# Layer norms between attention units: a subtraction and multiplication moved to GpSimd, its quarters set three half chunks apart

## The chip, the cores and the metric

The kernel runs on one core of a Trainium2 chip. The metric is the device time of one execution in microseconds (us), as the median of several runs. Durations inside the execution are from one profiled execution of the kernel before.

## What is computed

Two transformer layers over four sequences (batches) of 512 tokens with 320 features each. Every layer is self attention, cross attention on a context of 1601 tokens with 192 features, and a gated feed-forward part, each with a layer norm ahead and a residual behind. All is float32; there are 20 heads of 16 features.

```python
def _ln(x, g, b):
    m = jnp.mean(x, axis=-1, keepdims=True)
    v = jnp.mean(jnp.square(x - m), axis=-1, keepdims=True)
    return (x - m) * jax.lax.rsqrt(v + EPS) * g + b
...
h1 = _ln(x, n1_g, n1_b)
x = _attn(h1, h1, q1, k1, v1, o1_w, o1_b, heads) + x
h2 = _ln(x, n2_g, n2_b)
x = _attn(h2, context, q2, k2, v2, o2_w, o2_b, heads) + x
h3 = _ln(x, n3_g, n3_b)
proj = h3 @ ff_w1 + ff_b1
a, g = jnp.split(proj, 2, axis=-1)
ff = a * jax.nn.gelu(g, approximate=False) @ ff_w2 + ff_b2
return ff + x
```

## The kernel before

The attention work is cut into units: one layer, one kind (self or cross), one batch and one group of four heads, so five units a batch. A unit goes through its keys in **chunks** of 128: 4 chunks in self attention, 13 in cross attention (the last of 65 keys). For a chunk, TensorE makes the scores of the four heads (`st`, L1282, twelve matmuls with the row of negative maxima `nrows` as the third pass), ScalarE takes the exponentials (`pr`, L1292), TensorE multiplies them with the values one chunk later (`av`, L1308, four matmuls in the program, eight in the trace), ScalarE copies that out (`vo`, L1327) and GpSimd adds it to the unit's sum `o` (L1328). Since every query's maximum must be known before the exponentials, the scores of the **next** unit are made at the same time in another layout (`sps`, L1054, eight matmuls a chunk) and VectorE reduces them to maxima (`pm` and `nmax`, L1069, four a chunk). The two kinds of matmul use different rows of TensorE and run beside each other; products whose keys or queries have not been moved into place in time are left out of a chunk and made up later as a round of their own (`round_of(extra[0])`).

Everything else is fitted between the chunks by a planner that runs while the program is built: values (`vps`, L1015), keys of the context (`kps`, L951), queries (`qps`, L927), output projections (`ops`, L1211), and the norms. Each such step stands in a chain (a queue that is taken in order) with a cost, a due round, and two tests; one chunk advances the clock by two rounds, so a round is half a chunk. `pick` takes the chain whose head is due first, `steps` runs heads as credit allows and at most one or two steps marked `LIGHT` after a chunk. The planner also keeps an estimate of when each engine is free (`busy`), from which `bank` picks PSUM banks and `taken` picks VectorE or ScalarE for a copy out of PSUM.

A norm (`add_norm`) is such a list of steps in the chain "norm": `stats` (a quarter, 128 tokens, at a time), `root` (the inverse root, mostly on GpSimd), then for each quarter `normalise` (L562, 128x320, written to the only buffer `hn`) and `blocks` (L568, VectorE's transpose of 32x32 blocks from `hn` into `hturned`), then `spread`, which queues the DMAs (L578) that carry `hturned` to `hT`, one band each, on SyncE's queue; and in the chain "scale" `affine` (L595, GpSimd). Only then is `hT` handed over, and the step `hold` at the head of the projection chain waits for that; behind it in the same chain stand the queries of that batch's first unit and the keys and queries of the units after it. Three kinds of norm differ: with `first` set they take another path (`plain`, L608, and TensorE's transposes); feed-forward norms of the batches 1 to 3 run their quarters in pairs; all others go by `normalise` and `blocks` in one step per quarter. Before the change, a quarter's `normalise` is directly followed by its `blocks` on VectorE, four steps in four rounds.

`max_end` makes a unit's row of negative maxima at the end of the unit before; in cross attention its four DMAs (`rows`, L1133) are not issued at once but put at the head of a list of errands, which `carry` works off after a chunk.

Of the kernel before, what the change touches and what calls it, by code (L numbers as in the profile page):

```python
# [24 lines left out]
NQ = N // P  # L25
# [50 lines left out]
def kernel(ctx: ExitStack, tc: tile.TileContext, x, context, ws, out):  # L76
# [18 lines left out]
    nc = tc.nc  # L95
# [199 lines left out]
    class Unit:  # L295


        def __init__(self, l, kind, b, g):
            self.l, self.kind, self.b, self.g = l, kind, b, g
            self.cross = kind == "cross"  # L300
            self.nkeys = S2 if self.cross else N
            self.nch = (self.nkeys + P - 1) // P

            self.moves = {"k": deque(), "q": deque()}
            self.moving = {"k": 0, "q": 0}
            self.open = 6 if self.cross else 3
            self.keyed = None
            self.when = None
            self.vmade = [0, 0]

            self.made = {"q": 0, "k": 0, "kv": 0}
            self.scored = 0
            self.valued = 0
            self.steps = 2 * self.nch if kind != "ff" else 2 * NHC + NQ
            self.before = None
            self.others = []
            self.early = False
            self.own = {}
            self.pairs = self.hT = self.kvT = None
# [63 lines left out]
    clock = {"round": 0, "credit": 0.0, "lights": 0, "tiles": None, "ff": False}  # L383
    ALIKE = ("project", "early", "proj", "values")
    LIGHT = 0.01
# [26 lines left out]
    def busy(engine, us, *tiles):  # L412
        expect[engine] = max([expect[engine]] + [bank_of[id(t)][3] + 0.05 for t in tiles]) + us
        for t in tiles:
            bank_free[bank_of[id(t)][0]] = expect[engine] + 0.09
# [12 lines left out]
    def add(chain, cost, f, due, ready=yes, soon=yes):  # L428
        chains[chain].append((cost if isinstance(cost, tuple) else (cost,), due, ready, soon, f))
# [107 lines left out]
    def add_norm(l, b, i, put, done, due):  # L537
        xb = xs[b]
        s = {}

        def stats(t):
            if t == 0:
                hn_used.append(b)
                s["mv"] = two.tile([P, NQ, 2], F32, tag="mv", name="mv")
            st = three.tile([P, 6], F32, tag="st6", name="st6")
            nc.vector.bn_stats(st, xb[:, t, :])
            nc.vector.bn_aggr(s["mv"][:, t, :], st)
            busy("dve", 0.65)
# [9 lines left out]
        def normalise(t):  # L558
            if t == 0:
                s["turned"] = one.tile([P, DB, NQ, SLOT], F32, tag="hturned", name="hturned")  # L560
            s["hn"] = one.tile([P, D], F32, tag="hn", name="hn")
            nc.vector.tensor_scalar(  # L562
                s["hn"], xb[:, t, :], s["mv"][:, t, 0:1], s["rstd"][:, t : t + 1], ALU.subtract, ALU.mult,
            )
            busy("dve", 0.4)

        def blocks(t):
            nc.vector.transpose(s["turned"][:, :, t, :], s["hn"])  # L568
            busy("dve", 0.45)
            s["round"] = clock["round"]  # L570
# [66 lines left out]
        ahead = 0 if first or i == 2 and b else EARLIER  # L637
# [5 lines left out]
        def later(n, key="round"):  # L643
            return lambda: clock["round"] >= s[key] + n

        def together(f):
            return [lambda ts=ts: [f(t) for t in ts] for ts in (((0, 1), (2, 3)) if i == 2 and b else ((0,), (1,), (2,), (3,)))]
# [12 lines left out]
        if first:  # L660
# [5 lines left out]
                    may_overwrite if k == 0 else yes, later(1),  # L666
                )
            return
        for t, f in enumerate(together(lambda t: (normalise(t), blocks(t)))):
            add("norm", LIGHT, f, due - ahead - 13 + t, yes, yes if t else later(1))  # L670
        add("norm", 0.0, spread, due - ahead - 6, may_overwrite, later(1))

        def there(k):
# [106 lines left out]
    errands = deque()  # L780
# [333 lines left out]
    def max_end(u):  # L1114

        top, high, low = (u.nm[:, :, i, :] for i in range(3))
        nc.vector.tensor_reduce(
            high.bitcast(F32R), top.rearrange("p j (t o) -> p j t o", o=1), AX.X, ALU.max, negate=True
        )
        nc.vector.tensor_reduce(  # L1120
            low, u.nm[:, :, 0:2, :].rearrange("p j e t -> p j t e"), AX.X, ALU.add, negate=True
        )
        turned = two.tile([P, SLOT], F32, tag="turned", name="turned")

        nc.vector.transpose(turned.rearrange("p (j c) -> p j c", j=HG), u.nm[:, :, 1:3, :].rearrange("p j e t -> p j (e t)"))
        busy("dve", 0.6)
        slots = u.rows.bitcast(F32).rearrange("(g s) n -> s g n", s=DH)[0].rearrange("g (t r) -> g t r", t=NQ)

        def rows():
            for i in range(P // SLOT):  # L1130
                part = slice(i * SLOT, (i + 1) * SLOT)
                queue = (nc.sync, nc.scalar, nc.gpsimd, nc.sync)[i] if start["on"] else nc.sync
                queue.dma_start(out=slots[:, :, part], in_=turned[part, :])  # L1133

        if u.cross and u.before.cross:
            errands.appendleft((clock["round"] + 1, yes, rows))
        else:
            rows()
# [133 lines left out]
    def main(u, give, nxt):  # L1272

        pr, raised = {}, {}

        def score(c, j):
            r = min(P, u.nkeys - c * P)
            rows = slice(j * SLOT, (j + 1) * SLOT)
            own = []

            def product(e):
                nc.tensor.matmul(  # L1282
                    own[0][:r, :],
                    lhsT=ones[rows, :r] if e == 2 else u.keys(rows, c),
                    rhs=u.rows[rows, :] if e == 2 else u.q[rows, e, :],
                    start=(e == 0),
                    stop=(e == 2),
                )

            def exponential():  # L1290
                p = prs.tile([P, N], F32, tag="pr", name="pr")
                nc.scalar.activation(p[:r], own[0][:r], AF.Exp)  # L1292
                pr[c, j] = p
                busy("act", 0.515, *own)
                raised[c] = expect["act"]

            return (j,), [lambda e=e: product(e) for e in range(3)], exponential, own, lambda: own.append(bank("st"))
# [34 lines left out]
        for c in range(u.nch):  # L1332
# [29 lines left out]
            if not last and c == u.nch - 3:  # L1362
                max_reduce(nxt)
                max_end(nxt)
# [52 lines left out]
    def ff_main(u, give, nxt):  # L1417
        done = 0

        def beside(room, n):  # L1420

            nonlocal done
            if room:
                for extra in give(done, True)[1]:
                    round_of(extra)
            done += n
            if done == u.steps - 1 and nxt is not None and nxt.kind != "ff":
                max_reduce(nxt)
# [302 lines left out]
```

## Time and profile before

| | |
|---|---|
| Median of 3 runs | 2983.01 us (2982.85 to 2983.1) |
| Profiled execution, its time | 2982.2 us |
| Its span, first to last instruction | 2980.4 us |
| What lies around the span | 1.8 us |
| TensorE busy, share of the span | 2874.4 us, 96% |
| VectorE, ScalarE, GpSimd busy | 2119.6, 1889.8, 1193.4 us (71, 63, 40%) |
| Granted TensorE clock, mean | 0.994 |

Engines are named PE (TensorE), DVE (VectorE), ACT (ScalarE), POOL (GpSimd) and SP (SyncE, the DMA queue). A row of the timeline has the start in us from the span's begin, the duration, engine, line, operation, the tiles written and read, a count if like instructions are merged, and in brackets how long the engine had been idle and what ended that. A row of a grouped view has the count, then busy us and mean ns of one, then the idle time ahead with its causes.

### The profile page before, as it was taken

How to read it: one execution, taken by the hardware profiler on the slowest of the kernel's cores; microseconds unless marked ns; L12 is line 12 of the kernel's file. 1: busy time of each engine (PE TensorE's matmuls, PEld its weight loads, DVE VectorE, ACT ScalarE, POOL GpSimd, SP SyncE). 2: the span in 40 equal slices, each digit the busy share in tenths (PEclk: the TensorE clock that was granted, in tenths of full speed). 3: DMA queues.
4: the chain of work that ended last, by engine and by line, in shares of the span. 5: the costliest groups of instructions: out<-in, count | busy, mean ns of one | idle time of the engine just before them, and what ended most of it. 6: DMA issues, size and time to landing. Idle time of an engine off the chain costs nothing.

```text
span 2980.4 us, 84363 instructions
## 1 busy us (share of the span) xinstructions
PE 2874.4 (96%) x35018; PEld 1511.5 (51%) x35018; DVE 2119.6 (71%) x4143; ACT 1889.8 (63%) x3746; POOL 1193.4 (40%) x1305
## 2 busy tenths in 40 slices
PE   8999999999999999999999899999999999999999
PEld 4455555555554555355554555555555555544555
DVE  7877888889889888323268778888898888873221
ACT  3766677877877878501137676778878778784000
POOL 3445344554544545211224443445445454451110
PEclk8999999999999999999999999999999999999999
DMA  4443233132132122200123342221221121222000
GB/s 105 104 125 97 71 80 95 49 89 60 48 91 68 39 56 61 83 17 14 38 60 73 92 100 68 61 61 48 62 64 46 49 71 42 55 56 77 23 22 14
DMA packets 186543, 188.70 MB, mean 63 GB/s; under 512 B 69668, under 2 KB 137264, under 8 KB 186160
## 3 DMA queue, kind: packets, MB, share of 16 engines
q1 hardware_dynamic: 185368, 182.11, 24.2%
q8 instruction: 276, 4.52, 0.6%
q10 hardware_dynamic: 760, 1.18, 0.2%
q14 instruction: 107, 0.88, 0.1%
q0 software_dynamic: 32, 0.00, 0.0%
HBM read 55.76 MB, written 29.36 MB: 29 GB/s over the span
## 4 chain that ended last, share of the span: by engine, by line
PE 79%; DVE 16%; ACT 1%; DMA 1%; issue 1%; POOL 1%; SPq 0%; ACTq 0%; POOLq 0%; DVEq 0%
PE av L1308 22%; PE st L1282 16%; PE fps L1393 9%; DVE pm L1069 8%; PE sps L1054 6%; PE yps L1500 6%; PE vps L1015 5%; DVE nmax L1069 4%; PE kps L951 4%; PE ops L1211 3%; PE qkps L886 3%; PE fps L1453 2%; PE qps L927 2%; PE sps L1081 1%; ACT pr L1292 1%; DVE hturned L608 1%
## 5 line engine op out<-in xcount | busy, mean ns | idle before, releaser
L1292 ACT ACTIVATE pr<-st 128x512 f32<-128x512 f32 (+1 forms) x2720 | 1405.1, 603 | 418.3 <-PE st L1282 382.4
L1069 DVE TENSOR_REDUCE pm<-sps 128x1 f32<-128x512 f32 x1920 | 1187.2, 682 | 136.3 <-PE sps L1054 125.8
L1328 POOL TENSOR_TENSOR o<-o,vo 128x512 f32<-128x512 f32 x576 | 740.3, 1285 | 1101.8 <-ACT vo L1327 1091.9
L1054 PE MATMUL sps<-kT,q 32*128 32x512 f32 x4800 | 866.5, 429 | 12.2 <-DMA q<-low 3.2
L1308 PE MATMUL av<-pr,vals 128*32 128x512 f32 (+1 forms) x5440 | 735.1, 606 | 72.3 <-DVE nmax L1069 18.5
L1282 PE MATMUL st<-q,kT 32*128 32x512 f32 (+1 forms) x5120 | 791.6, 421 | 1.3 <-DVE pm L1069 0.8
L1282 PEld LDWEIGHTS st<-q,kT 32*128 32x128 f32 (+1 forms) x5120 | 420.7, 180 | 289.7 <-issue 119.1
L1282 PE MATMUL st<-nrows,ones 32*128 32x512 f32 (+1 forms) x2720 | 542.5, 400 | 8.5 <-DMA nrows<-turned 8.5
L1054 PEld LDWEIGHTS sps<-kT,q 32*128 32x128 f32 x4800 | 423.4, 184 | 93.3 <-DVE nmax L1069 15.7
L1069 DVE TENSOR_REDUCE nmax<-sps 128x1 f32<-128x512 f32 x640 | 395.7, 681 | 85.9 <-PE sps L1054 83.0
L1327 ACT COPY vo<-av 128x512 f32<-128x512 f32 x576 | 352.4, 612 | 20.9 <-PE av L1308 19.9
L1464 ACT ACTIVATE gl<-fps,b 128x512 f32<-128x512 f32 x80 | 54.8, 687 | 414.3 <-PE fps L1453 303.0
L1308 PEld LDWEIGHTS av<-pr,vals 128*32 128x32 f32 (+1 forms) x5440 | 111.1, 108 | 347.2 <-DVE pm L1069 179.4
L1393 PE MATMUL fps<-hT,w 128*128 128x512 f32 x640 | 283.2, 597 | 0.0
L1282 PEld LDWEIGHTS st<-nrows,ones 32*128 32x128 f32 (+1 forms) x2720 | 246.7, 180 | 33.2 <-issue 7.2
L1465 DVE SCALAR_TENSOR_TENSOR hid<-fps,b,gl 128x512 f32<-128x512 f32 x80 | 59.7, 748 | 238.8 <-ACT gl L1464 236.7
L1393 PEld LDWEIGHTS fps<-hT,w 128*128 128x128 f32 x640 | 119.2, 190 | 155.1 <-issue 151.8
L1500 PE MATMUL yps<-w,hid 128*128 128x320 f32 x640 | 176.0, 435 | 0.1
L1500 PEld LDWEIGHTS yps<-w,hid 128*128 128x128 f32 x640 | 120.4, 190 | 56.5 <-ACT gl L1464 5.3
L1211 PEld LDWEIGHTS ops<-wo,aT 112*32 112x32 f32 (+1 forms) x3072 | 97.7, 110 | 64.1 <-issue 42.9
L1211 PE MATMUL ops<-wo,aT 112*32 112x160 f32 (+1 forms) x3072 | 125.9, 300 | 0.9 <-DVE pm L1069 0.7
L886 PE MATMUL qkps<-hT,wqk 96*32 96x256 f32 (+1 forms) x1920 | 121.3, 395 | 0.0
(89 smaller groups left out, 2340.2 us busy)
## 6 DMA issues: line engine op xcount, KB each, us to landing
kT<-stages SPq DMA_DIRECT2D x160, 200.2 KB
oway<-o SPq DMA_DIRECT2D x80, 256.0 KB
q<-high SPq DMA_DIRECT2D x160, 64.0 KB
q<-low SPq DMA_DIRECT2D x160, 64.0 KB
kT<-high SPq DMA_DIRECT2D x60, 128.0 KB
q<-high SPq DMA_DIRECT2D x60, 128.0 KB
kT<-low SPq DMA_DIRECT2D x57, 128.0 KB
aT<-oway SPq DMA_DIRECT2D x32, 224.0 KB
```

The source lines that it names most:

```text
L886: nc.tensor.matmul(ps[f : f + m, :w], lhsT=wqk[:n, k, f // GD, column : column + m], rhs=first.hT[:n, k, at : at + w], start=(k == 0), sto ...
L1015: nc.tensor.matmul(ps[f : f + m, :w], lhsT=u.kvT[:n, k, at + f : at + f + m], rhs=wv[:n, k, h0 * DH : h1 * DH], start=(k == 0), stop=(k == ...
L1054: nc.tensor.matmul(ps, lhsT=u.q[j * SLOT : (j + 1) * SLOT, e, t * P : (t + 1) * P], rhs=u.kT[j * SLOT : (j + 1) * SLOT, u.k0 + s * 512 : u ...
L1069: nc.vector.tensor_reduce(to[:, j : j + 1], ps, AX.X, ALU.max)
L1211: nc.tensor.matmul(ps[f : f + m, : D // 2], lhsT=aT[:n, k, f * NQ + t * SLOT : f * NQ + t * SLOT + m], rhs=wo[:n, k, cols], start=(k == 0) ...
L1282: nc.tensor.matmul(own[0][:r, :], lhsT=ones[rows, :r] if e == 2 else u.keys(rows, c), rhs=u.rows[rows, :] if e == 2 else u.q[rows, e, :], ...
L1292: nc.scalar.activation(p[:r], own[0][:r], AF.Exp)
L1308: nc.tensor.matmul(ps[j * SLOT : (j + 1) * SLOT, :], lhsT=columns_of[:r, head : head + SLOT], rhs=pr.pop((c, j))[:r, :], start=True, stop= ...
L1327: nc.scalar.copy(vo, ps)
L1328: nc.gpsimd.tensor_tensor(u.o, u.o, vo, ALU.add)
L1393: nc.tensor.matmul(ps, lhsT=w1[:, k, i * FF + c * P : i * FF + (c + 1) * P], rhs=natural(u.hT[:, k]), start=start, stop=stop,)
L1500: nc.tensor.matmul(ps[:, :D], lhsT=hid[c][:, t * P : (t + 1) * P], rhs=w2[:, c, :], start=(c == 0), stop=(c == NHC - 1),)
```

## The change

For cross attention's norms of the batches 1 to 3 and the feed-forward norm of batch 0, in both layers (eight norms, `alone` false), `normalise` goes to GpSimd. It becomes a step of its own, free of charge and not `LIGHT`, due three rounds after the one before; `blocks` is a step of its own, due two rounds behind its `normalise` and held until two rounds have passed. `spread` follows as before. The estimate for VectorE is no longer charged for the moved instruction. Besides, a unit's `rows` still waiting among the errands is carried out at the latest when its `main` begins.

```diff
@@ def add_norm
+        alone = i == 2 and b > 0 or i == 0
...
             s["hn"] = one.tile([P, D], F32, tag="hn", name="hn")
-            nc.vector.tensor_scalar(
+            (nc.vector if alone else nc.gpsimd).tensor_scalar(
                 s["hn"], xb[:, t, :], s["mv"][:, t, 0:1], s["rstd"][:, t : t + 1], ALU.subtract, ALU.mult,
             )
-            busy("dve", 0.4)
+            if alone:
+                busy("dve", 0.4)
+            s["round"] = clock["round"]
...
-        for t, f in enumerate(together(lambda t: (normalise(t), blocks(t)))):
-            add("norm", LIGHT, f, due - ahead - 13 + t, yes, yes if t else later(1))
+        if alone:
+            for t, f in enumerate(together(lambda t: (normalise(t), blocks(t)))):
+                add("norm", LIGHT, f, due - ahead - 13 + t, yes, yes if t else later(1))
+        else:
+            for t in range(NQ):
+                add("norm", 0.0, lambda t=t: normalise(t), due - ahead - 17 + 3 * t, yes, later(1))
+                add("norm", LIGHT, lambda t=t: blocks(t), due - ahead - 15 + 3 * t, yes, later(2))
         add("norm", 0.0, spread, due - ahead - 6, may_overwrite, later(1))
@@ def max_end
         if u.cross and u.before.cross:
+            u.rows_of = rows
             errands.appendleft((clock["round"] + 1, yes, rows))
@@ def main
         pr, raised = {}, {}
+        for todo in [e for e in errands if e[2] is u.rows_of]:
+            errands.remove(todo)
+            todo[2]()
```

What this does to the order on the engines, at three places. (Lines of the changed kernel are counted in its own file: its L564, L572, L1003, L1063, L1078, L1228, L1295, L1321, L1341 are L562, L568, L994, L1054, L1069, L1218, L1282, L1308, L1328 of before.)

VectorE at the norm of batch 2 ahead of layer 0's cross attention, before; `hn` is the normalised quarter, `hturned` its transposed blocks, `pm<-sps` the reductions of a chunk:

```order
L994 COPY vals<-vps 128x12x16
L733 STREAM_TRANSPOSE stages<-stages 128x6x32
L562 TENSOR_SCALAR hn<-x_109,mv,root_12657 128x320
L568 STREAM_TRANSPOSE hturned<-hn 128x10x32
L1069 TENSOR_REDUCE pm<-sps 128x1 x4
L562 TENSOR_SCALAR hn<-x_109,mv,root_12657 128x320
L568 STREAM_TRANSPOSE hturned<-hn 128x10x32
L1069 TENSOR_REDUCE pm<-sps 128x1 x4
L994 COPY vals<-vps 128x12x16
L562 TENSOR_SCALAR hn<-x_109,mv,root_12657 128x320
L568 STREAM_TRANSPOSE hturned<-hn 128x10x32
L1069 TENSOR_REDUCE pm<-sps 128x1 x4
```

And VectorE at the same norm after the change:

```order
L742 STREAM_TRANSPOSE stages<-stages 128x6x32
L1078 TENSOR_REDUCE pm<-sps 128x1 x4
L572 STREAM_TRANSPOSE hturned<-hn 128x10x32
L1228 TENSOR_TENSOR x_107<-ops,x_107 128x160
L1078 TENSOR_REDUCE pm<-sps 128x1 x8
L572 STREAM_TRANSPOSE hturned<-hn 128x10x32
L1078 TENSOR_REDUCE pm<-sps 128x1 x4
L1003 COPY vals<-vps 128x12x16
L1078 TENSOR_REDUCE pm<-sps 128x1 x4
L1003 COPY vals<-vps 128x12x16
L572 STREAM_TRANSPOSE hturned<-hn 128x10x32
L1078 TENSOR_REDUCE pm<-sps 128x1 x4
```

`hn` is gone from VectorE, and the transposes stand two chunks (eight reductions) apart where they stood one apart.

GpSimd at the same norm after the change; `o<-o,vo` is the addition of one chunk, `high` and `low` belong to a query's move:

```order
L1341 TENSOR_TENSOR o<-o,vo 128x512
L564 TENSOR_SCALAR hn<-x_109,mv,root_12609 128x320
L1341 TENSOR_TENSOR o<-o,vo 128x512 x2
L564 TENSOR_SCALAR hn<-x_109,mv,root_12609 128x320
L812 COPY high<-low 128x256
L813 TENSOR_TENSOR low<-low,high 128x256
L1341 TENSOR_TENSOR o<-o,vo 128x512 x2
L564 TENSOR_SCALAR hn<-x_109,mv,root_12609 128x320
L1341 TENSOR_TENSOR o<-o,vo 128x512 x2
L564 TENSOR_SCALAR hn<-x_109,mv,root_12609 128x320
```

Each `hn` stands right behind a chunk's addition, and there are two additions from one `hn` to the next; the transposition of a quarter stands behind the four reductions of the following chunk.

TensorE late in the cross attention of batch 0 in layer 0, before, one chunk; `sps<-kT_135,q_104` are the products for the maxima of batch 1's first unit, whose queries come out of the first changed norm:

```order
L1308 MATMUL av<-pr,vals 32x512 x4
L951 MATMUL kps<-ctxT,w_116 32x200 x8
L1282 MATMUL st<-q_102,kT_134 128x512 x2
L1054 MATMUL sps<-kT_135,q_104 128x512 x2
L1282 MATMUL st<-q_102,kT_134 128x512 x2
L1054 MATMUL sps<-kT_135,q_104 128x512 x2
L1282 MATMUL st<-nrows_98,ones 128x512 x2
L1282 MATMUL st<-q_102,kT_134 128x512 x4
L1054 MATMUL sps<-kT_135,q_104 128x512 x2
L1282 MATMUL st<-nrows_98,ones 128x512 x2
L1054 MATMUL sps<-kT_135,q_104 128x512 x2
```

The same place after the change, this chunk and the two behind it:

```order
L1321 MATMUL av<-pr,vals 32x512 x4
L1295 MATMUL st<-q_102,kT_134 128x512 x8
L1295 MATMUL st<-nrows_98,ones 128x512 x4
L1321 MATMUL av<-pr,vals 32x512 x4
L1295 MATMUL st<-q_102,kT_134 65x512 x8
L1295 MATMUL st<-nrows_98,ones 65x512 x4
L1321 MATMUL av<-pr,vals 32x512 x4
L1295 MATMUL st<-q_103,kT_101 128x512 x8
L1295 MATMUL st<-nrows_97,ones 128x512 x4
```

Three chunks have lost their `sps` products; they come back as a second set of eight in three later chunks. The queries of that batch (`qps`) stand three chunks later than before. At the same norm of layer 1 it is one chunk that loses them and one that has sixteen. On the DMA queue, the four DMAs of `nrows`, which stood between the DMAs of `hT` in these norms, now stand ahead of them.

More of the change, by code (lines that the diff above doesn't have):

```diff
@@ L300, in __init__ @@
             self.cross = kind == "cross"
+            self.rows_of = None
             self.nkeys = S2 if self.cross else N
```

## The prediction

> **What bounds the kernel now.** I read the page first, then the chain of waits inside eight stretches, then the timeline of one of them engine by engine.
>
> ```profile
> PE 2874.4 (96%) x35018; PEld 1511.5 (51%) x35018; DVE 2119.6 (71%) x4143; ACT 1889.8 (63%) x3746; POOL 1193.4 (40%) x1305
> PE 79%; DVE 16%; ACT 1%; DMA 1%; issue 1%; POOL 1%; SPq 0%; ACTq 0%; POOLq 0%; DVEq 0%
> ```
>
> TensorE is the bound: 2980.4 - 2874.4 = 106 us of the span are all that it is idle. VectorE has 16% of the chain that ended last, so where TensorE waits it is mostly VectorE that it waits for, and an instruction taken from VectorE is worth something only in chunks where VectorE falls behind. How the moved instruction and the transposition that stays behave over the whole run (min/median/max in ns):
>
> ```profile
> L562 DVE TENSOR_SCALAR hn<-x,mv,root x64: 426/446/1507, 496.7 to 2876.6; 128x320 f32<-128x320 f32 x64
> L568 DVE STREAM_TRANSPOSE hturned<-hn x64: 510/511/513, 497.1 to 2877.1; 128x320 f32<-128x320 f32 x64
> ```
>
> The transposition takes 0.51 us always. `hn` takes 0.43 to 1.51 us, the same work each time. The timeline of GpSimd and then of VectorE at the norm of batch 2 in layer 0 shows why:
>
> ```profile
> 704.64 1.29 POOL L1328 TENSOR_TENSOR o<-o,vo 128x512 f32<-128x512 f32 x1
> ...
> 708.41 1.29 POOL L1328 TENSOR_TENSOR o<-o,vo 128x512 f32<-128x512 f32 x1 [2.48 <-ACT vo L1327]
> ```
>
> ```profile
> 704.84 1.27 DVE L562 TENSOR_SCALAR hn<-x,mv,root 128x320 f32<-128x320 f32 x1
> ...
> 708.95 0.93 DVE L562 TENSOR_SCALAR hn<-x,mv,root 128x320 f32<-128x320 f32 x1
> ...
> 710.35 2.44 DVE L1069 TENSOR_REDUCE pm<-sps 128x1 f32<-128x512 f32 x4
> ```
>
> The first `hn` began 0.20 us into GpSimd's addition and ended at 706.11, 0.18 us behind its end (705.93); the second began 0.54 us into the next one and ended 0.18 us behind it (709.88 against 709.70). `hn` waits on VectorE until GpSimd's addition is over, with four reductions queued behind it. What that costs TensorE, by the starts of its `av` matmuls, one group a chunk:
>
> ```profile
> 706.44 1.06 PE L1308 MATMUL av<-pr,vals 128*32 128x512 f32 x8 [0.22 <-ACT pr L1292]
> ...
> 711.05 1.07 PE L1308 MATMUL av<-pr,vals 128*32 128x512 f32 x8 [0.89 <-DVE pm L1069]
> ...
> 714.35 1.06 PE L1308 MATMUL av<-pr,vals 128*32 128x512 f32 x8 [0.22 <-ACT pr L1292]
> ...
> 718.24 1.07 PE L1308 MATMUL av<-pr,vals 128*32 128x512 f32 x8
> ```
>
> The three chunks last 4.61, 3.30 and 3.89 us. The first and the third hold `qps` and `ops` beside the usual matmuls. The same chunks where no norm runs, first with `qps`, then with `ops`:
>
> ```profile
> 539.56 1.06 PE L1308 MATMUL av<-pr,vals 128*32 128x512 f32 x8
> ...
> 543.38 0.64 PE L1308 MATMUL av<-pr,vals 128*32 128x512 f32 x4
> ```
>
> ```profile
> 384.08 1.06 PE L1308 MATMUL av<-pr,vals 128*32 128x512 f32 x8
> ...
> 387.42 1.07 PE L1308 MATMUL av<-pr,vals 128*32 128x512 f32 x8
> ```
>
> They last 3.82 and 3.34 us, so this norm costs 0.79 + 0.55 = 1.3 us.
>
> **What goes.** Eight norms lose four `hn` each. For all eight stretches together (busy us, the second row for L562 alone):
>
> ```profile
> sum 130.00, PE 119.06 PEld 58.54 DVE 126.01 ACT 95.25 POOL 58.90; mean PE 14.88 PEld 7.32 DVE 15.75 ACT 11.91 POOL 7.36
> ```
>
> ```profile
> sum 130.00, DVE 27.13; mean DVE 3.39
> ```
>
> 27.1 us leave VectorE, which is busy for 126.0 of the 130. TensorE is idle there for 130.00 - 119.06 = 10.9 us: the lower bound of what they cost. It is not all, since matmuls that are held up in their middle count as busy, so I take the lengths of the chunks. The worst chunk of the first norm and of the last, and a bare chunk (nothing beside scores, products and `av`) for comparison:
>
> ```profile
> 502.47 1.07 PE L1308 MATMUL av<-pr,vals 128*32 128x512 f32 x8
> ...
> 507.05 0.64 PE L1308 MATMUL av<-pr,vals 128*32 128x512 f32 x4
> ```
>
> ```profile
> 2620.69 1.07 PE L1308 MATMUL av<-pr,vals 128*32 128x512 f32 x8
> ...
> 2625.50 1.07 PE L1308 MATMUL av<-pr,vals 128*32 128x512 f32 x8
> ```
>
> ```profile
> 582.62 1.06 PE L1308 MATMUL av<-pr,vals 128*32 128x512 f32 x8
> ...
> 585.35 0.64 PE L1308 MATMUL av<-pr,vals 128*32 128x512 f32 x4
> ```
>
> The first is a bare one: 4.58 instead of 2.73, 1.85 too long. The last holds one `vps` of 192 columns, as the one from 711.05 does: 4.81 instead of 3.30, 1.51 too long. Subtracting so, chunk by chunk, the norms cost 2.1, 1.3, 1.6, 2.2, 2.0, 1.7, 1.8 and 2.2 us, together **-14.9 us** if all of it goes.
>
> **What stays.** The 32 transpositions stay on VectorE, now two chunks apart. What such a load costs is seen just ahead of the first norm:
>
> ```profile
> 492.98 0.36 DVE L994 COPY vals<-vps 128x192 f32<-128x192 f32 x1
> 493.26 0.37 DVE L733 STREAM_TRANSPOSE stages<-stages 128x192 f32<-128x192 f32 x1
> 494.27 2.48 DVE L1069 TENSOR_REDUCE pm<-sps 128x1 f32<-128x512 f32 x4 [0.65 <-PE sps L1054]
> ```
>
> With 0.7 us beside its reductions VectorE still had to wait 0.65 us for TensorE: nothing lost. Only in a bare chunk do 2.44 + 0.51 = 2.95 us exceed its 2.73, by 0.2; about one cross chunk in five or six is bare, so six of 32 make **+1.2 us**. From above: if the transpositions go on costing what norm work costs now, 14.9 us for 27.1 busy us of `hn` and 32 x 0.51 = 16.4 of transposing, it is 0.34 x 16.4 = 5.6. From below, nothing.
>
> **What GpSimd gets.** The trace has no 128x320 `TENSOR_SCALAR` there, but two others:
>
> ```profile
> L595 POOL TENSOR_SCALAR hT<-hT,lng,lnb 128x512 f32<-128x512 f32 x32 | 24.7, 772 | 127.6 <-DMA hT<-hturned 116.0 <-PE ops L1211 11.6
> L513 POOL TENSOR_SCALAR root<-root 128x4 f32<-128x4 f32 x22 | 5.1, 231 | 258.2 <-DVE root L507 257.9
> ```
>
> Between 0.23 and 0.77; on the line through both it is 0.57 us, 18 us in all. GpSimd was idle 2.48 us ahead of the addition at 708.41, so I cost it at **0**. An `hn` behind that addition would end at 709.70 + 0.57 = 710.27, and the transposition stands behind the next four reductions, which ended at 712.79, or with VectorE no longer late some 1.2 us sooner (they could start when their products do): a cover of 1.3 to 2.5 us.
>
> **What is moved.** The last quarter is turned some four chunks later, so `spread`, the twelve DMAs of `hT` (sixteen for feed-forward), `affine`, and with them `hold`, come later too. Most norms have room for it; the first cross norm of each layer has not. There the queries come three chunks later in layer 0, and three chunks lose their products for the maxima, which return as a second set in three later chunks; in layer 1 it is one. What one costs, by a chunk that lost them, then one that has a second set and the one behind it, then an ordinary chunk with the same `vps` of 128 columns:
>
> ```profile
> 766.58 1.07 PE L1308 MATMUL av<-pr,vals 128*32 128x512 f32 x8
> 768.47 1.07 PE L1308 MATMUL av<-pr,vals 128*32 128x512 f32 x8
> ```
>
> ```profile
> 395.11 1.06 PE L1308 MATMUL av<-pr,vals 128*32 128x512 f32 x8
> ...
> 399.34 1.06 PE L1308 MATMUL av<-pr,vals 128*32 128x512 f32 x8
> ...
> 402.92 1.06 PE L1308 MATMUL av<-pr,vals 128*32 128x512 f32 x8
> ```
>
> ```profile
> 533.64 1.06 PE L1308 MATMUL av<-pr,vals 128*32 128x512 f32 x8
> ...
> 536.60 0.64 PE L1308 MATMUL av<-pr,vals 128*32 128x512 f32 x4
> ```
>
> The second set with its aftermath costs 7.81 - 2 x 2.96 = 1.89. The chunk without gives back 2.73 - 1.89 = 0.84 if it stands alone, but little when three stand in a row, because ScalarE needs its time for them:
>
> ```profile
> 768.57 2.07 ACT L1292 ACTIVATE pr<-st 128x512 f32<-128x512 f32 x4
> 770.50 0.62 ACT L1327 COPY vo<-av 128x512 f32<-128x512 f32 x1
> ```
>
> 2.07 + 0.62 = 2.69, as long as a bare chunk. So four at 1.05 to 1.89 are 4.2 to 7.6 us; three of the four stand in a row, so I take **+6.0**. The other shifts exchange the places of `vps`, `kps` and `ops` chunk for chunk, at zero.
>
> **The row of maxima.** Its four DMAs now go ahead of those of `hT`, which delays no one, and once, in batch 0 of layer 0, ahead of the last loads of the division; there TensorE waited for them. All eight such waits:
>
> ```profile
> PE st L1282 <- DMA nrows<-turned: 8.5, 8, 2.4
> ```
>
> One of eight is worth at most about 1.1 us and at least nothing; I take **-0.5**. The flush in `main` changes nothing else in the order.
>
> **The sum** is -14.9 + 1.2 + 0 + 6.0 - 0.5 = -8.2 us, made against the profiled execution: 2980.4 us of span and 1.8 around it are 2982.2, and become 2974.0. The median of the runs lies 0.8 us higher (2983.0), so I forecast **2974.8 us**. With each term at its better bound it is 2971.2 (-14.9 + 0 + 4.2 - 1.1), at its worse 2985.3 (-10.9 + 5.6 + 7.6).
>
> **The rivals.**
> - *The late products cost nothing*, because the chunks with a second set fall where TensorE's other work hides it: -14.9 + 1.2 - 0.5, 2968.8 us. For it speaks that such chunks with `qps` or `ops` in the next absorb part; against it the 1.89 measured, and that the heavy chunks are now bunched ahead of them. 0.12.
> - *The stall stays in part*: only TensorE's visible idle time comes back (-10.9) and the transpositions keep 5.6: 2983.2 with the order's 6.0. For it: VectorE is 97% busy in these stretches, and it loses only 27.1 of 126.0. 0.18.
> - *Slower: the transposition waits for GpSimd.* VectorE works in order; behind the transposition stand four reductions, behind these TensorE's next products. If GpSimd delivers `hn` late, by a burst of additions and the splits of 1.2 to 2.5 us that stand in the same queue, every late us goes to TensorE. 32 delays of 0.26 us eat the 8.2 us, 0.44 us each make it 2989. Against it: the cover of 1.3 us or more. 0.08, at 2990.
> - *The load is only moved, the interference with it.* Then the 14.9 does not come, the order's 6.0 and 18 us of GpSimd work do: about 2989. Against it: the 64 transpositions, many of them beside GpSimd's work, all took 0.51 us, so what remains on VectorE there does not wait for GpSimd. 0.05. The Trainium skill, Perfetto Trace Analysis, section Optimizing Scalar/DVE Operations, speaks for this rival: it says that VectorE and GpSimd share a read port, and that offloading from the one to the other might therefore not help; by that rule the time would be this 2989. The trace agrees with the sharing (`hn` ends 0.18 us behind the addition), but what is moved here is the very instruction that waits.
>
> That the instruction would not be moved is excluded by the order.
>
> **How the numbers follow.** The forecast's case has a chance of 0.55, the four rivals 0.43, and 0.02 is left for what I don't see. About 0.2% (6 us) is what a measurement of this kernel can tell from no change: faster means below 2977.0. Of the forecast's case three quarters lie there, of the first rival all, of the second a sixth: 0.41 + 0.12 + 0.03 = 0.56. Slower by 6 us are most of the last two and what is left: 0.11. Within: 0.33. The range of 8 in 10 takes in the first rival at its low end and the second at its high end: 2968.5 to 2983.5.
>
> **What would show it.** In the profile after, no `hn` on VectorE in the eight stretches and 32 on GpSimd at 0.5 to 0.6 us; the chunk with `qps` at batch 2 down from 4.61 to some 3.8 us; TensorE's idle time there down by 10 us. At the first cross norm of layer 0, three chunks without `sps`, 2 to 2.7 us each, and three of 4.3 us. Wrong would be: waits of VectorE's transposition for GpSimd's `hn`; chunks of the norms still over 4 us; or a long wait of `sps` for the DMAs of queries and keys behind the first norm, which I have put at nothing since those products are only taken two chunks after the DMAs' issue.

## The result, and the profile after

The changed kernel takes 2973.13 us (median of 7 runs, 2967.84 to 2974.48), the kernel before beside it 2982.85 (7 runs): a ratio of 0.9966, 95% interval 0.9954 to 0.9977, 9.7 us less. The forecast was 2974.8. The total was right, but two of the terms that make it up were wrong by 4.5 and 6 us, in opposite directions, and so was the reason given for the largest.

TensorE still bounds: 99.4 us of the span are all that it is idle, 106 before (busy us and share of the span by engine):

```profile
span 2971.5 us, 84372 instructions
...
PE 2872.1 (97%) x35018; PEld 1511.8 (51%) x35018; DVE 2088.6 (70%) x4103; ACT 1891.4 (64%) x3754; POOL 1239.0 (42%) x1337
```

The moved normalisation (min/median/max in ns), and below it what the transpositions waited for (us, times):

```profile
L564 POOL TENSOR_SCALAR hn<-x,mv,root x32: 1428/1440/1453, 498.8 to 2630.8; 128x320 f32<-128x320 f32 x32
...
  POOL hn L564: 1.0, 3
```

On GpSimd it takes 1.44 us, two and a half times my estimate, and costs next to nothing all the same: 29 of 32 transpositions found it done. The norm of batch 2 in layer 0, on GpSimd, VectorE and TensorE:

```profile
708.77 1.29 POOL L1341 TENSOR_TENSOR o<-o,vo 128x512 f32<-128x512 f32 x1 [1.84 <-ACT vo L1340]
710.04 1.45 POOL L564 TENSOR_SCALAR hn<-x,mv,root 128x320 f32<-128x320 f32 x1
```

```profile
711.63 0.50 DVE L572 STREAM_TRANSPOSE hturned<-hn 128x320 f32<-128x320 f32 x1
...
719.44 0.50 DVE L572 STREAM_TRANSPOSE hturned<-hn 128x320 f32<-128x320 f32 x1
```

```profile
713.96 1.06 PE L1321 MATMUL av<-pr,vals 128*32 128x512 f32 x8
717.78 1.06 PE L1321 MATMUL av<-pr,vals 128*32 128x512 f32 x8
720.51 1.06 PE L1321 MATMUL av<-pr,vals 128*32 128x512 f32 x8
```

The chunk that lasted 4.61 us before lasts 3.82 (713.96 to 717.78), what such a chunk takes without a norm. The one behind it is bare and holds a transposition: 2.73, as without. So transpositions that stand alone cost nothing here; I had 1.2 us for them. In eight windows laid over the norms TensorE is now idle for 127.00 - 123.13 = 3.9 us, 10.9 before, so 7 us less where I had said 10:

```profile
sum 127.00, PE 123.13 PEld 64.64 DVE 105.49 ACT 98.67 POOL 87.29; mean PE 15.39 PEld 8.08 DVE 13.19 ACT 12.33 POOL 10.91
```

One chunk of these norms is still over 4 us, which the prediction named as a sign of being wrong: 4.13 from 508.31, where TensorE itself has two rounds of `vps` to do.

The whole difference of the two profiles, by the starts of the `av` groups (chunk by chunk, the same 680 in both; us, after minus before). A norm's stretch reaches from some ten chunks ahead of its first normalisation to some ten behind; other ends move the sum of the eight by up to 0.8 us:

| Part of the program | us |
|---|---|
| The eight norms: layer 0 batch 1, 2, 3, feed-forward; then layer 1 | -2.5, -2.2, -1.4, -3.4; -2.4, -2.1, -2.1, -2.7: -18.7 |
| The 45 chunks behind the first cross norm of layer 0 | +9.8 |
| The 42 chunks behind that of layer 1 | +1.4 |
| Behind the six other norms | +0.5 |
| Where nothing was changed | -1.9 |
| Sum | -8.9 |

The norms gave more than the 13.7 us forecast; the place where the queries come late took more than the 6.0. There, at the very spot that I had said "delays no one", TensorE stands still. TensorE, SP's queue, and the windows around it (after the busy times of the five engines comes the granted clock):

```profile
561.85 1.41 PE L1321 MATMUL av<-pr,vals 128*32 128x512 f32 x8
566.78 0.80 PE L1295 MATMUL st<-nrows,ones 32*128 32x512 f32 x4 [2.86 <-DMA nrows<-turned]
567.51 1.94 PE L1321 MATMUL av<-pr,vals 65*32 65x512 f32 x8
...
573.94 1.06 PE L1321 MATMUL av<-pr,vals 128*32 128x512 f32 x8
```

```profile
558.49 0.60 SPq L861 DMA_DIRECT2D q<-low  x1
559.19 3.65 SPq L861 DMA_DIRECT2D kT<-stages  x4
562.93 2.69 SPq L1142 DMA_DIRECT2D nrows<-turned  x4
```

```profile
564.00:567.00 3.00, 0.22 (x4) 0.25 (x4) 0.00 (x0) 1.03 (x3) 2.07 (x2) 0.85 0.30 57
567.00:570.00 3.00, 3.00 (x20) 0.87 (x24) 0.00 (x0) 2.42 (x5) 0.00 (x0) 0.50 0.00 0
570.00:573.00 3.00, 3.00 (x32) 1.48 (x28) 0.00 (x0) 0.59 (x2) 1.67 (x2) 0.51 0.05 10
573.00:576.00 3.00, 2.87 (x41) 1.46 (x35) 2.77 (x5) 2.54 (x5) 0.74 (x1) 1.00 0.35 71
```

The row of maxima stands behind the late queries and keys in SP's queue; its DMAs start at 562.93, and TensorE waits 2.86 us for them. Then the clock falls to half for 6 us, which by that costs about 3 more, an estimate: `av` takes 1.94 us. The two chunks last 5.66 and 6.43 us.

### The profile page after: what moved, and what is told of

The parts are those of the page before. It is cut to its first block, busy times and chain, and to the rows that moved or that the text cites. A ratio compares the mean times of both kernels' runs of the same rounds, so it can differ in the third digit from the quotient of the medians.

```text
span 2971.5 us, 84372 instructions
## 1 busy us (share of the span) xinstructions
PE 2872.1 (97%) x35018; PEld 1511.8 (51%) x35018; DVE 2088.6 (70%) x4103; ACT 1891.4 (64%) x3754; POOL 1239.0 (42%) x1337
## 4 chain that ended last, share of the span: by engine, by line
PE 80%; DVE 14%; DMA 2%; ACT 1%; issue 1%; SPq 1%; POOL 1%; ACTq 0%; POOLq 0%; DVEq 0%
PE av L1321 22%; PE st L1295 16%; PE fps L1406 9%; DVE pm L1078 8%; PE sps L1063 6%; PE yps L1513 6%; PE vps L1024 5%; DVE nmax L1078 4%; PE kps L960 4%; PE ops L1221 3%; PE qkps L895 3%; PE fps L1466 2%; PE qps L936 2%; PE sps L1090 1%; DVE hturned L612 1%
## 5 line engine op out<-in xcount | busy, mean ns | idle before, releaser
L1078 DVE TENSOR_REDUCE pm<-sps 128x1 f32<-128x512 f32 x1920 | 1188.2, 681 | 161.4 <-PE sps L1063 152.4
L1341 POOL TENSOR_TENSOR o<-o,vo 128x512 f32<-128x512 f32 x576 | 740.5, 1286 | 1054.3 <-ACT vo L1340 1018.9
L1063 PE MATMUL sps<-kT,q 32*128 32x512 f32 x4800 | 863.0, 429 | 9.7 <-DMA q<-low 3.2
L1321 PE MATMUL av<-pr,vals 128*32 128x512 f32 (+1 forms) x5440 | 737.5, 608 | 66.7 <-DVE nmax L1078 18.8
L1295 PE MATMUL st<-q,kT 32*128 32x512 f32 (+1 forms) x5120 | 787.2, 421 | 0.6
L1295 PEld LDWEIGHTS st<-q,kT 32*128 32x128 f32 (+1 forms) x5120 | 420.3, 180 | 290.7 <-issue 125.1
L1295 PE MATMUL st<-nrows,ones 32*128 32x512 f32 (+1 forms) x2720 | 540.5, 399 | 11.2 <-DMA nrows<-turned 11.2
L1063 PEld LDWEIGHTS sps<-kT,q 32*128 32x128 f32 x4800 | 423.6, 184 | 86.8 <-DVE nmax L1078 15.8
L1078 DVE TENSOR_REDUCE nmax<-sps 128x1 f32<-128x512 f32 x640 | 395.2, 680 | 88.1 <-PE sps L1063 83.4
L1321 PEld LDWEIGHTS av<-pr,vals 128*32 128x32 f32 (+1 forms) x5440 | 111.4, 108 | 342.3 <-DVE pm L1078 183.7
L1295 PEld LDWEIGHTS st<-nrows,ones 32*128 32x128 f32 (+1 forms) x2720 | 246.5, 180 | 35.9 <-DMA nrows<-turned 7.5
```

Of the source, the lines that this page charges most:

```text
L1063: nc.tensor.matmul(ps, lhsT=u.q[j * SLOT : (j + 1) * SLOT, e, t * P : (t + 1) * P], rhs=u.kT[j * SLOT : (j + 1) * SLOT, u.k0 + s * 512 : u ...
L1078: nc.vector.tensor_reduce(to[:, j : j + 1], ps, AX.X, ALU.max)
L1295: nc.tensor.matmul(own[0][:r, :], lhsT=ones[rows, :r] if e == 2 else u.keys(rows, c), rhs=u.rows[rows, :] if e == 2 else u.q[rows, e, :], ...
L1321: nc.tensor.matmul(ps[j * SLOT : (j + 1) * SLOT, :], lhsT=columns_of[:r, head : head + SLOT], rhs=pr.pop((c, j))[:r, :], start=True, stop= ...
L1341: nc.gpsimd.tensor_tensor(u.o, u.o, vo, ALU.add)
```

## The experiments

Three questions: what the place behind the first cross norm costs and why; whether the engine or the place in the program made the gain; what GpSimd's work costs. Each run is compared with runs of the kernel before on the same chip:

| Run | Median, us | Ratio to before (95%) | Eight norms, by chunks, us |
|---|---|---|---|
| changed kernel | 2973.1 | 0.9966 (0.9954 to 0.9977) | -18.7 |
| rows_ahead | 2965.6 | 0.9946 (0.9932 to 0.9960) | -18.7 |
| early3 | 2960.7 | 0.9927 (0.9915 to 0.9940) | -18.1 |
| skip_first | 2965.0 | 0.9943 (0.9930 to 0.9955) | -10.9 |
| spread_only | 2974.4 | 0.9976 (0.9967 to 0.9985) | -16.0 |
| move_only | 3044.3 | 1.0207 (1.0193 to 1.0221) | +66.0 |
| early_vector | 2964.9 | 0.9944 (0.9932 to 0.9957) | -11.2 |
| early_together | 2982.7 | 1.0003 (0.9994 to 1.0012) | -0.2 |
| early_double | 2965.1 | 0.9944 (0.9930 to 0.9957) | -12.8 |
| early_fma | 2958.2 | 0.9919 (0.9906 to 0.9933) | -18.7 |
| no_addition | 2941.4 (one) | | -13.3 |

The last column is against the profile of before, as in the table above.

### What the late queries cost: rows_ahead, early3, skip_first

rows_ahead puts the row of maxima ahead of waiting keys in the queue; in the whole program four DMAs change places with four:

```diff
...
         for _, what, u in sorted(movers):
+            if what == "k" and errands and errands[0][2] in maxima and clock["round"] >= errands[0][0]:
+                errands.popleft()[2]()
...
```

> The changed kernel with eight DMAs in another order, once in the program: behind the first cross norm of layer 0 the row of maxima's four DMAs go ahead of the four of the keys. Theory (there the late queries and keys fill SP's queue, the maxima land 2.9 us after TensorE needs them, and the idle time is followed by some 6 us at half the clock, about 3.3 us more): 6.2 us less than the changed kernel's 2973.1, so 2967, no wait of st for nrows over 1 us at that place, and no slow clock behind it. Rival (the bunched late products alone cost the time there, the wait only stands where TensorE would wait for ScalarE anyway): 2973. Second rival (the keys, now later, are waited for instead): 2972 or more, with a wait of sps for kT.

Its two chunks in question, the queue, and the window that ran at half the clock:

```profile
561.07 1.41 PE L1325 MATMUL av<-pr,vals 128*32 128x512 f32 x8
...
563.67 1.21 PE L1325 MATMUL av<-pr,vals 65*32 65x512 f32 x8
...
567.65 0.64 PE L1325 MATMUL av<-pr,vals 128*32 128x512 f32 x4
```

```profile
559.35 2.69 SPq L1145 DMA_DIRECT2D nrows<-turned  x4
562.15 2.53 SPq L864 DMA_DIRECT2D kT<-stages  x4
```

```profile
567.00:570.00 3.00, 3.00 (x39) 1.66 (x33) 2.94 (x5) 2.56 (x6) 2.09 (x3) 1.00 0.11 16
```

The chunks last 2.60 and 3.98 us, 5.5 less together, the clock stays at 1.00, no one waits for the keys, and the 45 chunks cost +4.2 instead of +9.8. The theory holds. The 4.2 are the late products themselves.

early3 makes the first cross norm of each layer three half chunks sooner; by the order, no products are late any more:

```diff
-        ahead = 0 if first or i == 2 and b else EARLIER
+        ahead = 0 if first or i == 2 and b else EARLIER + 3 * (i == 1 and b == 1)
```

> The changed kernel with the norm of the first cross batch of each layer due three half chunks sooner; by the order no chunk loses its products for the maxima any more. Theory (everything that this place costs, 9.8 us in layer 0 and 1.4 in layer 1 by the chunks of the two profiles, comes from the queries being late): 2973.1 - 11.2 = 2962. Rival (late products cost nothing, only the one wait for the row of maxima does): 2967. Second rival (the norm's steps, now among other steps, stall there): 2970 or more, with chunks over 4 us in the norm's stretch.

Measured 2960.7. The 45 chunks cost 0.0, the 42 in layer 1 0.1, and the norms gain what they gained. skip_first takes the other way out and leaves these two norms as they were:

```diff
-        alone = i == 2 and b > 0 or i == 0
+        alone = i == 2 and b > 0 or i == 0 or i == 1 and b == 1
```

> The changed kernel without the change for the first cross batch of each layer: their normalisations stay on VectorE in the old places, so their queries are in time. Theory (each of these two norms gains 2.4 us in its own stretch and costs more behind it, 9.8 and 1.4 us): 2973.1 + 4.9 - 11.2 = 2966.8. Rival (what is seen behind them is chance, or would be there anyway): 2978.

Measured 2965.0, as the theory has it. For these two norms the change as it was made is a loss: undoing it there brings 8 us by the medians, 7 by the ratios.

### The engine or the place: spread_only, move_only, early_vector, early_together

spread_only has the new steps, but the normalisation on VectorE:

```diff
-            (nc.vector if alone else nc.gpsimd).tensor_scalar(
+            nc.vector.tensor_scalar(
...
-            if alone:
-                busy("dve", 0.4)
+            busy("dve", 0.4)
```

> The changed kernel with the normalisation back on VectorE, in the new places (quarters three half chunks apart, transposition two later). Theory (what held TensorE up is the normalisation on VectorE waiting for GpSimd's addition): the 32 go on taking 0.43 to 1.5 us, 0.85 on average; with 2.44 us of reductions they overrun a bare chunk by some 0.5 us and fit into the others, about 8 us in all over the changed kernel: 2981. Rival (it was the four quarters in a row that stalled, whichever engine has them): 2973, as the changed kernel.

Measured 2974.4, 1.3 over the changed kernel (the intervals overlap): this is what the rival says, which I had not even considered in the prediction. 16.0 of the 18.7 us come without any work leaving VectorE. The 32 normalisations in question, first in the kernel before (layer 0, then layer 1), then here:

```profile
L562 DVE TENSOR_SCALAR hn<-x,mv,root x16: 427/888/1494, 496.7 to 1144.1; 128x320 f32<-128x320 f32 x16
L562 DVE TENSOR_SCALAR hn<-x,mv,root x16: 426/670/1507, 1974.2 to 2621.4; 128x320 f32<-128x320 f32 x16
```

```profile
L564 DVE TENSOR_SCALAR hn<-x,mv,root x16: 425/437/1519, 500.6 to 1164.8; 128x320 f32<-128x320 f32 x16
L564 DVE TENSOR_SCALAR hn<-x,mv,root x16: 435/439/1385, 1975.9 to 2638.4; 128x320 f32<-128x320 f32 x16
```

The medians fall from 888 and 670 to 437 and 439 ns; over half a microsecond took 18 of the 32 before, and 4 here. Alone in its chunk, the normalisation starts before GpSimd's addition of that chunk: all 28 short ones do. Where more stands ahead of it, it starts later and meets the addition: the interference was a consequence of the pile as much as its cause.

move_only does the other half alone: on GpSimd, but each transposition directly behind, in the old places.

```diff
-        if alone:
+        if True:
             for t, f in enumerate(together(lambda t: (normalise(t), blocks(t)))):
```

> The engine alone: the 32 normalisations on GpSimd, but the steps as in the kernel before, each transposition directly behind its normalisation, quarters not spread. Theory (the place in the program made the gain, and the transposition stands in VectorE's order and waits for GpSimd, 1.44 us and whatever is ahead there, where VectorE itself took 0.85 on average): 0.6 us or more for each of 32 on top of what the norms cost before, about 2990 to 3003. Rival (taking the normalisation from VectorE is what gains, wherever it stands): 2968.

Measured 3044.3, 63 us over before in its own comparison (2981.4), in the direction of the theory and far beyond its range:

```profile
DVE hturned L572 <- POOL hn L564: 80.5, 32, 5.3
```

All 32 transpositions wait, 2.5 us on average, with four reductions queued behind each: 1.44 for the instruction, the rest for what stands ahead of it on GpSimd. So the slower rival of the prediction is real; only the distance of two half chunks keeps it away.

early_vector is spread_only with early3's earlier norms, so that no late products blur it.

> The place alone, with the late products gone: normalisation on VectorE, quarters three half chunks apart, transposition two later, the first cross norm of each layer three half chunks sooner. Against the same on GpSimd (2960.7). Theory (spreading keeps VectorE in time, and then the normalisation seldom meets GpSimd's addition): only the few that still wait, 4 of 32 in the run before it, cost 1 us each or less: 2961 to 2964. Rival (the engine is worth what was forecast for it, 13.7 us): 2974.

Measured 2964.9, at the edge of the theory, and 4.2 over early3 (the two intervals overlap; chunk by chunk the norms differ by 6.9). What the engine is worth shows in the first quarter of a norm: six normalisations take over half a microsecond, each the first of its norm, and the two norms without one are no faster in early3. GpSimd, VectorE and TensorE in layer 0:

```profile
488.12 0.20 POOL L524 TENSOR_TENSOR root<-root,root 128x4 f32<-128x4 f32 x1
488.27 1.26 POOL L1340 TENSOR_TENSOR o<-o,vo 128x512 f32<-128x512 f32 x1
```

```profile
488.36 1.36 DVE L564 TENSOR_SCALAR hn<-x,mv,root 128x320 f32<-128x320 f32 x1 [0.99 <-POOL root L524]
```

```profile
485.63 1.06 PE L1320 MATMUL av<-pr,vals 128*32 128x512 f32 x8
490.70 1.06 PE L1320 MATMUL av<-pr,vals 128*32 128x512 f32 x8
```

The root is made on GpSimd, with the addition queued right behind it. VectorE waits 0.99 us for the root and starts 0.09 us after the addition has begun, so it waits for that too. The chunk lasts 5.07 us; in early3, with `hn` behind the root on GpSimd itself, it lasts 3.18 (486.16 to 489.34):

```profile
486.16 1.06 PE L1321 MATMUL av<-pr,vals 128*32 128x512 f32 x8
489.34 1.06 PE L1321 MATMUL av<-pr,vals 128*32 128x512 f32 x8
```

early_together keeps the quarters due three half chunks apart, but joins the two instructions of a quarter on VectorE again:

```diff
...
-                add("norm", 0.0, lambda t=t: normalise(t), due - ahead - 17 + 3 * t, yes, later(1))
-                add("norm", LIGHT, lambda t=t: blocks(t), due - ahead - 15 + 3 * t, yes, later(2))
+                add("norm", LIGHT, lambda t=t: (normalise(t), blocks(t)), due - ahead - 16 + 3 * t, yes, later(2) if t else later(1))
```

> Normalisation and transposition of a quarter together on VectorE again, but the quarters three half chunks apart; first norms three half chunks sooner. Theory (a quarter is 0.44 + 0.51 = 0.95 us, with 2.44 of reductions 3.4: over a bare chunk's 2.73 by 0.66, less over the others; VectorE makes up for it in the chunk behind, which has none): 2962 to 2966, so that two quarters in one chunk were what TensorE waited for. Rival (any chunk that VectorE overruns is lost): about 0.5 us for each of 32, 2976.

Measured 2982.7: all of the gain is gone, and my theory for this run with it; it is even above the rival's 2976. The due rounds say when a step is wanted, not when it is carried out: the quarters come out one to three chunks apart here (1.3 on average), where early_vector has them two apart each time, and so have the transpositions of the changed kernel. So the run changes the distance too. But the six later quarters that do stand two or three chunks behind the one before take 0.50 to 1.50 us, and early_vector's 24 later quarters 0.43 to 0.44: distance alone is not enough, the transposition has to be set apart as well. The third and fourth quarter of batch 3 in layer 0, three chunks and one chunk behind the one before, on VectorE, GpSimd and TensorE:

```profile
936.20 1.36 DVE L564 TENSOR_SCALAR hn<-x,mv,root 128x320 f32<-128x320 f32 x1
...
940.79 1.26 DVE L564 TENSOR_SCALAR hn<-x,mv,root 128x320 f32<-128x320 f32 x1
```

```profile
936.09 1.28 POOL L1339 TENSOR_TENSOR o<-o,vo 128x512 f32<-128x512 f32 x1 [2.08 <-ACT vo L1338]
```

```profile
934.00 1.07 PE L1319 MATMUL av<-pr,vals 128*32 128x512 f32 x8
938.73 1.06 PE L1319 MATMUL av<-pr,vals 128*32 128x512 f32 x8 [0.83 <-DVE pm L1076]
942.96 1.06 PE L1319 MATMUL av<-pr,vals 128*32 128x512 f32 x8
```

The third starts 0.11 us into the addition. Its chunk lasts 4.73 us and the next one, with the fourth, 4.23: VectorE does not make up in a chunk for the one before that it overran. In early_vector these two quarters take 0.44 us, in chunks of 3.18 and 3.21 (their other work is not quite the same). As in the kernel before, 18 of the 32 take over half a microsecond.

### How much of it was the waiting: no_addition

no_addition is the kernel before without GpSimd's addition; it leaves out the sum over the chunks:

```diff
-                nc.gpsimd.tensor_tensor(u.o, u.o, vo, ALU.add)
```

> The kernel before without the running addition on GpSimd (it leaves out the sum of the products over the chunks, 576 additions of 1.29 us), for the eight stretches of the norms alone. All 32 normalisations take 0.44 us on VectorE then, 13 us less in sum. Theory (VectorE is overrun by the pile of a quarter or two in one chunk, 0.95 us each, and meeting the addition makes it worse): the eight stretches lose some 8 to 10 us of what they cost, and the first norm, two quarters a chunk, still has chunks over 3.5 us. Rival A (the waiting for the addition is all of the stall): 14 us or more go, no bare chunk over 3 us. Rival B (the waiting is hidden, only the load counts): under 4 us go.

The eight stretches lose 13.3 us. Elsewhere this kernel loses some 0.02 us a chunk (0.88 in the 45 chunks behind the first norm), 3.0 for the 155 of the stretches, so that some 10 go to the norms, of the 18.2 that they cost (18.7 less the 0.5 behind them). Every normalisation takes under 0.45 us now (the row is layer 0's), but the first norm, two quarters a chunk, still has a chunk of 4.07:

```profile
L562 DVE TENSOR_SCALAR hn<-x,mv,root x18: 404/434/447, 488.6 to 1224.6; 128x320 f32<-128x320 f32 x18
```

```profile
494.14 1.06 PE L1308 MATMUL av<-pr,vals 128*32 128x512 f32 x8 [0.16 <-ACT pr L1292]
498.21 1.07 PE L1308 MATMUL av<-pr,vals 128*32 128x512 f32 x8
```

So the waiting for GpSimd was about half of the stall, the pile itself the rest.

### What GpSimd's work costs: early_double, early_fma

Both stand on early3. early_double adds a second instruction of the same size:

```diff
+            if not alone:
+                nc.gpsimd.tensor_scalar(
+                    s["hn"], xb[:, t, :], s["mv"][:, t, 0:1], s["rstd"][:, t : t + 1], ALU.mult, ALU.add,
+                )
...
```

> The kernel with the first norms sooner, and on GpSimd ahead of each of the 32 normalisations a second instruction on the same operands, with multiplication and addition, whose result is overwritten. Theory (GpSimd's work is hidden: its cover, the time until the transposition stands at the head of VectorE's order, is over 2 us): 2960.7, within 2 us, and the transposition waits for GpSimd in a few cases only. Rival (GpSimd's work is on the path, or holds VectorE up by the shared access): another 0.5 to 1.4 us for each of 32, 2977 or more.

```profile
L565 POOL TENSOR_SCALAR hn<-x,mv,root x32: 599/608/627, 490.9 to 2620.8; 128x320 f32<-128x320 f32 x32
L568 POOL TENSOR_SCALAR hn<-x,mv,root x32: 1432/1434/1450, 491.6 to 2621.5; 128x320 f32<-128x320 f32 x32
...
  POOL hn L568: 14.3, 22
```

Measured 2965.1, between the two theories. With 0.61 us more, 22 transpositions wait 14.3 us in all; with 1.44 alone, 6 wait 3.2 us in early3 and 3 wait 1.0 in the changed kernel. The cover is there, but not the 2 us or more that I stated: it ends little beyond 1.44. early_fma makes the instruction shorter, by multiplying and adding:

```diff
...
+                if t == 0:
+                    s["mr"] = two.tile([P, NQ], F32, tag="mr", name="mr")
+                    nc.gpsimd.tensor_tensor(s["mr"], s["mv"][:, :, 0], s["rstd"], ALU.mult)
+                    nc.gpsimd.tensor_scalar(s["mr"], s["mr"], -1.0, None, ALU.mult)
+                nc.gpsimd.tensor_scalar(
+                    s["hn"], xb[:, t, :], s["rstd"][:, t : t + 1], s["mr"][:, t : t + 1], ALU.mult, ALU.add,
+                )
...
```

> The kernel with the first norms sooner, and the normalisation on GpSimd in another form: multiplied by the root and the product of mean and root, negated, added, from two small instructions once a norm. In the run with doubled work this form took 0.61 us where the other takes 1.43. Theory (GpSimd's work costs only what exceeds its cover, and at 1.44 us that is 1 us in all): 2960.7, 2959 to 2962, with no wait of a transposition for GpSimd. Rival (GpSimd's work costs in proportion, 4.4 us for the 19.5 us that the doubling added): 26 us less on GpSimd give 6 us, 2955.

```profile
L573 POOL TENSOR_SCALAR hn<-x,root,mr x32: 602/610/623, 489.3 to 2613.6; 128x320 f32<-128x320 f32 x32
...
  POOL hn L573: 0.4, 2
```

Measured 2958.2, just below the theory's range (2959 to 2962) and above the rival's 2955; the interval (0.9906 to 0.9933) overlaps early3's. By chunks the norms gain 0.6 us over early3, so the theory is the likelier; the two were not told apart. It is the best version run, 25 us under the kernel before in its own comparison (2983.4).

## Why the prediction was right, step by step

- **What bounds, and where.** Right: TensorE waits for VectorE in these eight stretches, and `hn` waits for GpSimd's addition. That waiting alone is worth 10 of the 18 us (no_addition).
- **What goes, -14.9.** It was 18.2, by the stretches and what lies behind them, against -13.7 for this term and the next together; my subtraction of like chunks took too little at each norm but one, most at the feed-forward norm of layer 0 (3.4, not 2.2). The reason was wrong in the step "27.1 us leave VectorE". I priced the change as one thing, the removal, where it had two parts; spread_only shows that setting the steps apart gives 16.0 us with all the work still on VectorE. The move adds 2.7 to it in the changed places and 6.9 in the earlier ones, through the root and the addition that the first quarter no longer meets.
- **What stays, +1.2.** Nothing: a bare chunk with a transposition lasted 2.73.
- **GpSimd, 0.** Right in effect, from a wrong duration: 1.44 us, not 0.57. The line that I drew ran through instructions without a subtraction, and early_fma's 0.61 lies near it; the form with a subtraction does not. With 1.44 the stated cover of 1.3 to 2.5 us was nearly used up.
- **Late products, +6.0.** Right: 4.2 in layer 0 and 1.4 in layer 1 (rows_ahead).
- **The row of maxima, -0.5.** Wrong, by 6 us. It "delays no one" by the order that I had read at another batch; behind the first cross norm of layer 0 it stands behind four DMAs of the keys that take 3.65 us. I had named a wait for late queries and keys as what would prove me wrong, and looked for it in `sps`; they were not waited for themselves but filled the queue ahead of something that was.
- **The rivals.** The Trainium skill (Perfetto Trace Analysis, section Optimizing Scalar/DVE Operations) doubts a move from VectorE to GpSimd since the two share a port; for that rival I had worked out 2989. The trace does not agree: with all else equal the move gains (early3 under early_vector, by 4.2 us in the medians and 6.9 in the eight norms). Waiting of the transposition for GpSimd is what the same move costs without the distance: 3044.

The sum came out by luck: -18.2 in place of -13.7 and +5.5 in place of -0.5 nearly cancel, and the 1.5 us that they leave are made up by 1.9 where the program is unchanged. Of these, 3.1 us less lie at one wait for `nrows` near 1826 us, 2.36 us with a slow clock behind it in the profile of before and 0.97 after, and 1.2 more elsewhere. Left open: whether that is more than chance was not tried. What the planner's new order of the other steps does inside the eight stretches was not taken apart from the norms. Nor was a kernel tried with the normalisation on VectorE in a place a little behind its root, which might do without GpSimd.

## What to carry to other kernels

Before moving work from an engine that is late, try to set it apart: two short instructions in one chunk, with the quarters closer together by it, cost more than the same two in two chunks (early_together against early_vector, for 32: 11.0 us in the stretches of the norms, 0.3 us a time, and 17.8 in the medians, of which the part outside the stretches was not explained). An overrun was not made up for, and later instructions came into another engine's way. A change with two parts is priced as two. Whoever makes a step later has to follow every DMA that it issues into its queue, and ask what stands behind it there, not only who waits for it.

## What the runs showed of the hardware

A short idle time of TensorE can cost as much again in clock. Two waits of the changed kernel for the row of maxima, each with the window that follows (granted clock third from the end):

```profile
177.04 0.79 PE L1295 MATMUL st<-nrows,ones 32*128 32x512 f32 x2 [2.41 <-DMA nrows<-turned]
```

```profile
177.00:180.00 3.00, 2.96 (x20) 1.30 (x24) 1.21 (x3) 2.06 (x4) 0.94 (x1) 0.50 0.88 199
```

```profile
1078.92 0.49 PE L1295 MATMUL st<-nrows,ones 32*128 32x512 f32 x2 [2.05 <-DMA nrows<-turned]
```

```profile
1080.00:1083.00 3.00, 2.92 (x44) 1.41 (x36) 2.37 (x5) 2.48 (x7) 0.96 (x1) 1.00 0.00 0
```

2.41 us halved the clock, as 2.86 did at 564; 2.05 did not, while in spread_only's profile 1.78 us did and in early_fma's 2.25 did not. So the length alone does not decide. The clock's records in the traces sort them: in each of the twelve, the slow spells begin on a grid of 3.41 us and last 3.41 us or a multiple of it, but for the last of each, which the end of the trace cuts off. From 100 us on, each wait of over 1.5 us that had 1.82 us or more within one step of its grid was followed by such a spell; of those that had less, some were and some were not. The 2.05 us lay in two steps, 1.24 and 0.81; early_fma's 2.25 were 1.67 and 0.59; spread_only's 1.78 lay in one. The Trainium skill (TensorE: Matmul & The Clock Gate, section What's actually happening) says that the clock halves after an idle window of about 3.4 us that runs freely; the grid agrees with the free window, the length does not: about half of one was enough here.

The form of an instruction matters on GpSimd: 128x320 with subtraction and multiplication 1.43 to 1.44 us, with multiplication and addition 0.61. And of VectorE and GpSimd the one that is clearly first goes through: in spread_only a normalisation that began 0.15 us ahead of the addition took 0.45 us, one that began only 0.05 us ahead of it 1.52.
